# A selective scan with its carry moved out of the scan: one bundle of changes to a Mamba and FFN layer on one core

## The chip, the cores and the metric

The kernel runs on one NeuronCore of one Trainium2 chip. The engines are named PE (matrix products; PEld is its weight load), DVE (the vector engine), ACT (the scalar engine), POOL (GpSimd) and SP (which only issues DMAs here). SBUF is the on-chip memory, PSUM the smaller one that PE writes its sums to; a tile is 128 partitions by so many columns. The metric is the device time of one execution in microseconds (us). Before the change it is 2003.3 us, the median of three runs (2002.98, 2003.30 and 2004.07).

## What is computed

The input x is [2, 4096, 256]. One layer is a state-space block with a residual, then an FFN with a residual, in fp32 throughout. Cut to what matters here:

```python
x_path, z = split(layernorm(x) @ W_in.T)      # 512 channels each
x_path = silu(x_path)
B, C, dt_in, lam_in = split(x_path @ W_x.T)   # 16 states
B, C = rope(rmsnorm(B + B_bias)), rope(rmsnorm(C + C_bias))
dt = softplus(dt_in * W_dt + b_dt)            # 512 channels
dA = exp(A * dt)                              # 512 channels x 16 states
u = (1 - lam) * dt * dA * Bx_prev + lam * dt * Bx    # Bx = B * x_path
h[t] = dA[t] * h[t-1] + u[t]                  # the scan, along 4096 tokens
y[t] = sum over states (h[t] * C[t])
y = (y + x_path * D) * silu(z)
x = x + layernorm(y @ W_out.T)
o = ffn(layernorm(x))       # ternary weights, gelu, an inner layernorm
x = x + layernorm(o)
```

The scan is the part that can't be cut along time: 2 batches x 512 channels x 16 states, each 4096 steps long.

## The kernel before, in words

Time is cut into blocks of 512 tokens, 8 to a batch, 16 in all (`k`). The 512 channels x 16 states of a block are laid out as 4 channel groups `j` x 4 state rounds `q` x 4 quarters `c`: a tile of 128 partitions holds 32 channels of quarter `c` for 4 states, and its 512 columns are the tokens. So a block has 64 units, each with one scan, and a batch's later blocks start their scans from the last state of the block before. Blocks 0 and 8 start a batch and have no carry.

For each unit:

- `decay` (L1036): ACT writes exp(A dt) into a PSUM tile `da`; there are 4 such buffers (`DA_PSUM`). The call is the helper at L230.
- `inputs` (L1041, the product with B): POOL multiplies the broadcast row b with the channel tile `vr` into the SBUF tile `g`, two quarters at a time (L1046). There are 3 buffers of g, one per (j, q) (`GBUFS`).
- `unit_scan` (L1052): DVE scans. Its start value is 0 in the first block of a batch and a column of `ini` otherwise. The first `SPLIT[q]` quarters (2, 1, 2, 1) are scanned into `da` in PSUM (L1059), the others into g (L1062).
- The product with C: for quarters in PSUM DVE does it, `product_v` (L1074, with a copy of the last state into `hl` at L1077); for quarters in g POOL does it in place, `product_g` (L1068, L1072). In place, it overwrites the last state, so `last` (L1064) has ACT copy that to `hl` first.
- `sum_states` (L1084): PE adds the 16 states of a channel into PSUM (L1088), which frees g. `start_y` puts the skip term there first, `gate` (DVE, L1098) multiplies with silu(z).

The carry: `over`, `over_x`, `spread` and `carry` (L943 to L1027) bring what the last token of the block before adds to this block's first inputs into `ini`; `initial` (POOL, L1032) adds the last states `hl`. It is called from the main loop, once for j = 0 and once for the rest.

Around the scan of block k run, on the same engines, the preparation of block k+1 (`plan_ahead`: norm, projections, dt, angles of the rotation, rotation, loads) and the output projection and FFN of block k-1 (`plan_behind`). At its end `ffn_scale` (ACT, L1220) scales the FFN's output by its norm's factor and `finish` (POOL, L1224) adds it to x, which is then stored.

The order of the work is written out by hand. `tc.manual_schedule()` keeps the program's order on each engine; each engine takes its instructions in that order and waits with semaphores. The main loop goes through the units, and each unit has three places (3 x unit, + 1, + 2); the scan stands between the second and the third. `AT` gives for each piece of the two plans the place, counted from the start of the current block (192 places a block), behind which it is written down; `AT_FIRST` does so for the first block's preparation, `W_AT` for the ternary weights, and `LAG` for the pieces that follow a unit (products, sums, gates) counts from the unit's own place. Decays and inputs come by `ahead`: at the middle place of each unit, decays are issued up to 2 units ahead and inputs too (`AHEAD_DA`, `AHEAD_U`). Loads of dt and v for channel group j+1 are issued when group j starts, and x two blocks on at unit 60 (`X_AT`). SP issues all block loads and stores from one queue, in that order as well.

The tiles b and c are two columns longer than the data, which starts at column 2, so that POOL's two inputs start 8 bytes apart modulo 32 bytes; the rows of g, before the change, have 512 columns and are written and read at the same address.

Of the kernel before, what the change touches and what calls it, by code (L numbers as in the profile page):

```python
# [8 lines left out]
F32 = mybir.dt.float32  # L9
# [5 lines left out]
P = 128  # L15
# [30 lines left out]
AHEAD_DA, AHEAD_U = 2, 2  # L46
X_AT = 60
# [4 lines left out]
    "product_v": (4,),  # L52
    "last": (24, 15, 21, 18, 13, 13, 18, 14, 19, 21, 21, 14, 15, 13, 19, 11),
    "product_g": (28, 17, 30, 19, 22, 17, 20, 26, 24, 21, 25, 20, 24, 13, 24, 15),
    "gate": (35, 38, 31, 26),
    "start": (18, 26, 27, 26),
    "sum": (32, 30, 36, 25, 36, 35, 24, 30, 31, 29, 28, 23, 45, 31, 29, 22),
}

W_AT = (1, 46, 70, 73, 74, 78, 85, 92, 103, 103, 106, 114, 116, 124, 141, 144, 149, 149, 153, 160, 160, 163, 163, 170, 174, 176, 180, 187, 188)  # L60
LOAD_FIRST = 6
AT = {
    "a_stats": (5, 5),
    "a_power": (5,),
    "a_offset": (8,),
    "a_apply": (8, 8),
    "a_turn": (15, 15),
    "a_evict": (16, 17),
    "project": (17, 24, 31, 31, 62, 66, 66, 76),
    "keep": (21, 25, 31, 35, 68, 72, 74, 78),  # L70
    "silu_x": (36,),
    "bc_project": (55, 60),
    "bc_take": (73,),
    "dt_project": (82,),
    "bc_square": (88,),
    "bc_power": (95,),
    "dt_row": (84,),
    "dt_spread": (92,),
    "softplus": (92,),
    "bc_scale": (137,),  # L80
    "dt_turn": (109, 115, 117, 117),
    "dt_keep": (117, 118, 118, 120),
    "dt_sum": (121,),
    "angles": (129,),
    "diag_lam": (118,),
    "silu_z": (153,),
    "sines": (153,),
    "rotate_a": (154,),
    "rotate_b": (154,),
    "bc_turn": (158,),  # L90
    "bc_store": (164,),
    "dot_sum": (176,),
    "dot_shift": (194,),
    "dot_take": (194,),
    "weigh": (141, 159, 194, 196),
    "weigh_x": (150, 167, 197, 197),
    "over": (121,),
    "over_x": (132,),
    "spread": (179,),
    "carry": (185,),  # L100
    "diag_dot": (196,),
    "skip": (198, 199, 199, 200),
    "skip_x": (198, 199, 200, 200),
    "load_dt": (124,),
    "load_v": (150,),
    "load_b": (167, 172, 172, 174),
    "load_c": (172, 184, 186, 189),
    "x_load": (4,),
    "out_project": (41, 49),
    "out_square": (47, 49),  # L110
    "out_power": (49, 54),
    "residual": (53, 54),
    "h_stats": (58, 58),
    "h_power": (63,),
    "h_offset": (65,),
    "h_apply": (68, 69),
    "h_turn": (78, 82),
    "h_evict": (78, 82),
    "ffn_1": (85, 93, 97, 98, 103, 107, 117, 129),
    "ffn_keep": (88, 94, 97, 106, 114, 115, 121, 135),  # L120
    "gelu": (133, 135),
    "ffn_2": (137, 150, 162, 190),
    "ffn_sums": (145, 159, 173, 191),
    "ffn_out": (146, 159, 175, 195),
    "ffn_square": (177, 160, 195, 196),
    "ffn_power": (180, 196),
    "ffn_scale": (189, 196),
    "finish": (189, 196),
# [3 lines left out]
    "a_stats": (-90, -90),  # L132
    "a_power": (-90,),
    "a_offset": (-90,),
    "a_apply": (-90, -90),
    "a_turn": (-90, -90),
    "a_evict": (-90, -90),
    "project": (-78, -77, -75, -72, 0, 12, 0, 3),
    "keep": (-76, -74, -71, -69, 0, 16, 0, 9),
    "silu_x": (-58,),  # L140
    "bc_project": (-70, -70),
    "bc_take": (-67,),
    "dt_project": (-66,),
    "bc_square": (-61,),
    "bc_power": (-60,),
    "dt_row": (-65,),
    "dt_spread": (-64,),
    "softplus": (-63,),
    "bc_scale": (-59,),
    "dt_sum": (-53,),  # L150
    "dt_turn": (-55, -55, -55, -55),
    "dt_keep": (-55, -55, -55, -55),
    "angles": (-52,),
    "diag_lam": (-54,),
    "silu_z": (56,),
    "sines": (-50,),
    "rotate_a": (-47,),
    "rotate_b": (-46,),
    "bc_turn": (-45,),
    "bc_store": (-44,),  # L160
    "dot_sum": (-30,),
    "dot_shift": (0,),
    "dot_take": (0,),
    "weigh": (-51, 0, 0, 2),
    "weigh_x": (-49, 0, 4, 8),
    "diag_dot": (0,),
    "skip": (1, 9, 0, 0),
    "skip_x": (2, 12, 0, 0),
    "load_dt": (-62,),
    "load_v": (-42,),  # L170
    "load_b": (-43, -20, 0, 7),
    "load_c": (-41, -20, 5, 20),
    "bc_project_first": (-73, -70, -69, -68),
    "decay_rates": (-57,),
# [4 lines left out]
def mamba_ffn_kernel(  # L179
# [374 lines left out]
    class Norm:  # L554


        def __init__(self, src, scale, eps, name):
            self.src, self.scale, self.eps, self.name = src, scale, eps, name
            self.mv = small.tile([P, NC4, 2], F32, tag="mv", name=f"mv_{name}")
            self.st = small.tile([P, NC4, 6], F32, tag="st", name=f"st_{name}")  # L560

        def stats(self, cs):
            for c in cs:
                nc.vector.bn_stats(self.st[:, c, :], self.src[:, c, :])
                nc.vector.bn_aggr(self.mv[:, c, :], self.st[:, c, :])
# [21 lines left out]
        def turn(self, kk):  # L587
            if kk == 0:
                self.oT = p1.tile([P, 2, T], F32, tag="oT", name=f"oT_{self.name}")
                self.pt = {}  # L590
# [1018 lines left out]
```

## Time and profile before

| what | value |
|---|---|
| median of three runs | 2003.3 us |
| span of the profiled execution | 2000.2 us (its own time beside it isn't given; the runs' median stands 3.1 us above the span) |
| one steady block (64 scans) | 116.5 us |
| first scan of block 0 / of block 1 | 59.8 / 196.1 us after the start |
| granted PE clock, mean | 0.953 |
| DVE: all 1024 scans | 1270 us of 1766 us busy |
| POOL: `inputs` and `product_g` | 1016 and 628 us of 1750 us busy |
| ACT: decays | 680 us of 1625 us busy |

How to read it. A profile line of a group gives the line in the kernel, the engine, the operation, the tile written and the tiles read (`out<-in`, buffer numbers left out), the shapes, how often it ran, then the busy time in us, the mean of one in ns, and the idle time of the engine just before these instructions with what ended most of it. Busy time that overlaps is counted once per group; neighbouring DVE instructions overlap by some 0.07 us. A line of a wait names who waited for whom, the us in total, the times and the longest. A line of the timeline is the start in us, the length in us, and the instruction. In the table of windows each engine has its busy us and its instructions in brackets; behind them stand the granted clock, the DMA engines' busy share and GB/s.

### The profile page before, as it was taken

The page shows a single profiled execution, that of the slowest core. Times are in us where ns is not written, and L with a number is a line of the kernel's source. Part 1 is how long each engine was busy: PE and PEld are TensorE (multiplying, and loading weights), DVE is VectorE, ACT ScalarE, POOL GpSimd, SP SyncE. Part 2 cuts the span into 40 slices and gives each one's busy share as a digit, 9 for nine tenths or more (in the row PEclk, how much of TensorE's full clock was granted, in tenths as well). Part 3 has the DMA queues.
Part 4 walks back from the last instruction along what each step waited for, and adds up shares of the span by engine and source line. Part 5 has one row for each costly group of instructions (what it writes and reads, how often), then busy time and mean ns, then how long its engine had stood idle before and what let it go on. Part 6 is the DMA issues. An engine that isn't in the chain of part 4 may idle for free.

```text
span 2000.2 us, 28645 instructions
## 1 busy us (share of the span) xinstructions
PE 1779.9 (89%) x8910; PEld 1058.4 (53%) x8910; DVE 1765.9 (88%) x2714; ACT 1625.3 (81%) x3511; POOL 1750.2 (88%) x1063
## 2 busy tenths in 40 slices
PE   6866999999999999999999999999999999998788
PEld 3433555464645546464554646455464645545257
DVE  1778989999898999999899999989999998999961
ACT  4766897979789797978979797988979798896754
POOL 3689999999899999999999999999999999999970
PEclk7876999999999999999999999999999999999898
DMA  5733446365354636545463644546364454635400
GB/s 98 194 85 100 113 113 169 79 153 123 101 123 112 166 78 155 126 102 122 113 170 86 157 111 109 126 113 162 85 160 106 113 125 111 161 85 149 85 21 11
DMA packets 155721, 233.41 MB, mean 117 GB/s; under 512 B 30160, under 2 KB 55824, under 8 KB 155568
## 3 DMA queue, kind: packets, MB, share of 16 engines
q1 hardware_dynamic: 153440, 230.80, 47.8%
q0 software_dynamic: 544, 0.71, 0.3%
q8 instruction: 70, 1.15, 0.3%
q14 instruction: 83, 0.68, 0.1%
q10 hardware_dynamic: 1584, 0.07, 0.1%
HBM read 188.51 MB, written 42.99 MB: 116 GB/s over the span
## 4 chain that ended last, share of the span: by engine, by line
DVE 41%; ACT 27%; PE 12%; issue 12%; POOL 3%; DMA 3%; SPq 0%; DVEq 0%; ACTq 0%; POOLq 0%
DVE g L1062 16%; DVE da L1059 12%; ACT da L230 7%; ACT L228 5%; DVE g L1076 4%; PE pf L1162 3%; ACT L230 2%; PE pz L644 2%; ACT dt L230 2%; POOL g L1046 2%; ACT zs L230 2%; DVE dx L989 1%; PE pf L1171 1%; DVE zs L1098 1%; ACT h L230 1%
## 5 line engine op out<-in xcount | busy, mean ns | idle before, releaser
L1046 POOL TENSOR_TENSOR g<-b,vr 128x1024 f32<-128x1024 f32 x512 | 1016.2, 2000 | 44.9 <-PE y L1088 22.5
L230 ACT ACTIVATE da<-dtr,aneg 128x512 f32<-128x512 f32 x1024 | 680.2, 681 | 33.6 <-DVE hl L1077 18.2
L1062 DVE TENSOR_TENSOR_SCAN g<-da,ini,g 128x512 f32<-128x512 f32 x560 | 688.4, 1267 | 19.8 <-ACT da L230 19.1
L1072 POOL TENSOR_TENSOR g<-c,g 128x1024 f32<-128x1024 f32 (+1 forms) x256 | 626.5, 2452 | 88.6 <-ACT hl L1066 69.1
L1059 DVE TENSOR_TENSOR_SCAN da<-da,ini,g 128x512 f32<-128x512 f32 x336 | 429.3, 1278 | 39.6 <-ACT da L230 32.9
L1088 PE MATMUL y<-g,fold 128*32 128x512 f32 x2048 | 339.7, 630 | 39.8 <-POOL g L1072 28.0
L1162 PE MATMUL pf<-w2q,h 128*128 128x257 f32 x1024 | 313.1, 387 | 15.5 <-DVE o L1200 11.8
L1076 DVE TENSOR_TENSOR g<-da,c 128x512 f32<-128x512 f32 x384 | 264.1, 688 | 17.6 <-DVE da L1059 0.5
L644 PE MATMUL pz<-oT_a,wi 128*128 128x512 f32 x512 | 243.3, 617 | 33.0 <-ACT zs L662 28.6
L1139 PE MATMUL ph<-oT_h,w1q 128*128 128x512 f32 x480 | 250.7, 654 | 22.0 <-ACT h L1150 17.1
L1171 PEld LDWEIGHTS pf<-h 128*128 128x128 f32 x1024 | 194.8, 190 | 26.9
L1171 PE MATMUL pf<-h 128*128 128x128 f32 x1024 | 196.9, 274 | 0.0
L1162 PEld LDWEIGHTS pf<-w2q,h 128*128 128x128 f32 x1024 | 155.2, 192 | 59.0 <-DVE o L1200 43.1
L644 PEld LDWEIGHTS pz<-oT_a,wi 128*128 128x128 f32 x512 | 91.5, 193 | 173.8 <-issue 74.3
L1139 PEld LDWEIGHTS ph<-oT_h,w1q 128*128 128x128 f32 x480 | 88.6, 202 | 178.5 <-issue 79.3
L1088 PEld LDWEIGHTS y<-g,fold 128*32 128x32 f32 x2048 | 53.3, 110 | 176.7 <-POOL g L1072 82.9
L1066 ACT COPY hl<-g 128x2 f32<-128x2 f32 (+1 forms) x256 | 47.0, 184 | 104.4 <-DVE g L1062 100.1
L228 ACT ACT_TABLE_LOAD x98 | 125.7, 1283 | 1.7
L1108 PE MATMUL po<-wo,zs 128*128 128x256 f32 x480 | 112.8, 389 | 0.0
L1108 PEld LDWEIGHTS po<-wo,zs 128*128 128x128 f32 x480 | 89.7, 192 | 37.1 <-ACT xp L662 11.8
L928 PE MATMUL ps<-dt,ident 128*128 128x511 f32 x128 | 73.0, 654 | 28.8 <-DVE remdot L890 25.1
L1062 DVE TENSOR_TENSOR_SCAN g<-da,g 128x512 f32<-128x512 f32 x80 | 93.7, 1207 | 2.7 <-ACT da L230 2.6
(232 smaller groups left out, 2460.2 us busy)
## 6 DMA issues: line engine op xcount, KB each, us to landing
dtr<-dt_d SPq DMA_DIRECT2D x256, 256.0 KB, 4.8
vr<-v_d SPq DMA_DIRECT2D x256, 256.0 KB, 7.3
dt_d<-dt SPq DMA_DIRECT2D x64, 256.0 KB, 2.1
v_d<-v SPq DMA_DIRECT2D x64, 256.0 KB, 2.8
b<-bc_d SPq DMA_DIRECT2D x256, 64.0 KB, 2.1
c<-bc_d SPq DMA_DIRECT2D x256, 64.0 KB, 2.2
xpre<-in_L_attn_x_dram SPq DMA_DIRECT2D x16, 512.0 KB, 4.4
xpost<-in_L_attn_x_dram SPq DMA_DIRECT2D x15, 512.0 KB, 4.6
```

Source lines behind the costliest of these rows:

```text
L228: nc.scalar.preload_act_table_set(name)
L230: nc.scalar.activation(dst, src, f, **kw)
L644: nc.tensor.matmul(s.pz[e], lhsT=wi[:, kk, e * P : (e + 1) * P], rhs=s.na.oT[:, kk, :], start=(kk == 0), stop=(kk == 1),)
L1046: nc.gpsimd.tensor_mul(s.g[j, q][:, hs, :], s.bcq[0, q][:, None, :].to_broadcast([P, 2, T]), s.ch[j, "vr"][:, hs, :],)
L1059: nc.vector.tensor_tensor_scan(da, da, g, ini, ALU.mult, ALU.add)
L1062: nc.vector.tensor_tensor_scan(g, da, g, ini, ALU.mult, ALU.add)
L1072: nc.gpsimd.tensor_mul(g, s.bcq[1, q][:, None, :].to_broadcast([P, NG - n, T]), g)
L1076: nc.vector.tensor_mul(s.g[j, q][:, c, :], da, s.bcq[1, q])
L1088: nc.tensor.matmul(s.ys[j][c * G : (c + 1) * G, :], lhsT=fold, rhs=g[:, c, :], start=False, stop=(q == NQ - 1), skip_group_check=True,)
L1139: nc.tensor.matmul(s.ph[f], lhsT=w1q[:, kk, f * P : (f + 1) * P], rhs=s.nh.oT[:, kk, :], start=(kk == 0), stop=(kk == 1),)
L1162: nc.tensor.matmul(po[:, 0 : DM + 1], lhsT=gT, rhs=w2q[:, f, :], start=(f == 0), stop=(f == NH - 1), skip_group_check=True,)
L1171: nc.tensor.matmul(po[:, DM + 1 :], lhsT=gT, rhs=gT, start=False, stop=False, skip_group_check=True,)
```

## The change

Seven things change together.

1. `inputs` makes all four quarters of a round in one POOL instruction of 128x4x512 instead of two.
2. The rows of g get 514 columns. `inputs` writes columns 2 to 513, the scan works there, and both products with C write columns 0 to 511, two columns ahead of what they read. Column 513, the last state, stays as it was, so `product_g` need not follow `last`.
3. Every scan starts from 0. A new piece `enter` (DVE) adds the carry to the first column of the four quarters before the scan, 16 times a block. For this the carry is multiplied with the first decay: `over_x` also copies the first dt, `spread` spreads it, `carry` makes `da0` from it (one DVE multiplication, one exponential), and `initial` has a second POOL multiplication.
4. `ffn_scale` is gone. `finish` is a DVE instruction a quarter of the block, which scales and adds at once, in place of ACT's scaling and POOL's addition.
5. `angles` is cut into 7 pieces with places of their own, the statistics of the norms are issued two by two, the four dt tiles are one.
6. Decays, inputs, `enter`, `initial`, the loads of dt and v and the load of the next x get places in the tables; `AHEAD_DA`, `AHEAD_U`, `X_AT` and `LOAD_FIRST` are gone.
7. Nearly all places in `LAG`, `AT`, `AT_FIRST` and `W_AT` are new.

The core of the diff:

```diff
-    def inputs(s, j, q, h):
-
-        if h == 0:
-            s.g[j, q] = scan.tile([P, NG, T], F32, tag="g", name=f"g_{s.k}_{j}_{q}", bufs=GBUFS)
-        hs = slice(2 * h, 2 * h + 2)
+    def inputs(s, j, q):
+
+        s.g[j, q] = scan.tile([P, NG, T + 2], F32, tag="g", name=f"g_{s.k}_{j}_{q}", bufs=GBUFS)
         nc.gpsimd.tensor_mul(
-            s.g[j, q][:, hs, :],
-            s.bcq[0, q][:, None, :].to_broadcast([P, 2, T]),
-            s.ch[j, "vr"][:, hs, :],
+            s.g[j, q][:, :, 2:],
+            s.bcq[0, q][:, None, :].to_broadcast([P, NG, T]),
+            s.ch[j, "vr"],
         )
 
+    def enter(s, j, q):
+
+        g0 = s.g[j, q][:, :, 2]
+        nc.vector.tensor_add(g0, s.ini[:, j, q, :], g0)
+
     def unit_scan(s, j, q, c):
 
-        da, g = das[s.k, j, q, c], s.g[j, q][:, c, :]
-        ini = 0.0 if s.first else s.ini[:, j, q, c : c + 1]
+        da, g = das[s.k, j, q, c], s.g[j, q][:, c, 2:]
...
-            nc.vector.tensor_tensor_scan(da, da, g, ini, ALU.mult, ALU.add)
+            nc.vector.tensor_tensor_scan(da, da, g, 0.0, ALU.mult, ALU.add)
...
-        nc.scalar.copy(s.hl[:, j, q, n:], s.g[j, q][:, n:, T - 1])
+        nc.scalar.copy(s.hl[:, j, q, n:], s.g[j, q][:, n:, T + 1])
...
-        nc.gpsimd.tensor_mul(g, s.bcq[1, q][:, None, :].to_broadcast([P, NG - n, T]), g)
+        nc.gpsimd.tensor_mul(
+            g[:, :, 0:T], s.bcq[1, q][:, None, :].to_broadcast([P, NG - n, T]), g[:, :, 2:]
+        )
...
-        nc.vector.tensor_mul(s.g[j, q][:, c, :], da, s.bcq[1, q])
+        nc.vector.tensor_mul(s.g[j, q][:, c, 0:T], da, s.bcq[1, q])
...
+        s.da0 = scan.tile([P, NJ, NQ, NG], F32, tag="da0", name=f"da0_{s.k}")
+        nc.vector.tensor_mul(s.da0, dt0[:, :, None, :].to_broadcast([P, NJ, NQ, NG]), aneg)
+        special(s.da0, s.da0, AF.Exp)
...
         nc.gpsimd.tensor_add(s.ini[:, js], s.ini[:, js], prev.hl[:, js])
+        nc.gpsimd.tensor_mul(s.ini[:, js], s.ini[:, js], s.da0[:, js])
...
-    def ffn_scale(s, h):
-        for i in range(2):
-            o = s.o2[:, 2 * h + i, :]
-            nc.scalar.activation(o, o, AF.Copy, scale=s.ff["rg", h][:, i : i + 1])
-
     def finish(s, h):
         hs = slice(2 * h, 2 * h + 2)
-        nc.gpsimd.tensor_add(s.x[:, hs, :], s.o2[:, hs, :], s.x[:, hs, :])
+        for i in range(2):
+            c = 2 * h + i
+            xc = s.x[:, c, :]
+            nc.vector.scalar_tensor_tensor(
+                xc, s.o2[:, c, :], s.ff["rg", h][:, i : i + 1], xc, ALU.mult, ALU.add
+            )
         nc.sync.dma_start(tokens(out, s.k)[:, hs, :], s.x[:, hs, :])
```

And of the places (after the change, in order of j, q and, for decays, c):

```diff
-AHEAD_DA, AHEAD_U = 2, 2
-X_AT = 60
...
+    "decay": (-3, -4, 0, -3, -7, 1, 1, 0, -2, -1, 0, 0, -1, 1, -17, -3, ...
+    "inputs": (-9, -2, -7, -2, -7, -19, -11, 1, -11, -6, -11, -2, -9, -11, -2, -8,),
+    "enter": (-1, 1, -3, -1, 1, 0, 0, 1, -3, -1, -2, 1, -1, 0, 1, -1,),
...
-    "product_g": (28, 17, 30, 19, 22, 17, 20, 26, 24, 21, 25, 20, 24, 13, 24, 15),
+    "product_g": (18, 19, 13, 17, 12, 20, 14, 13, 16, 19, 18, 11, 27, 14, 24, 13,),
...
-    "x_load": (4,),
+    "x_load": (33,),
...
+    "initial": (181, 220,),
+    "x_next": (185,),
-    "load_dt": (124,),
-    "load_v": (150,),
+    "load_dt": (149, 200, 232, 264,),
+    "load_v": (173, 224, 234, 274,),
```

## The prediction

> **What bounds the kernel now.** I read the busy times first, then one steady block, then the groups of instructions with shapes kept apart, then the waits, then the timeline where DVE and POOL meet.
>
> The page's head:
>
> ```profile
> span 2000.2 us, 28645 instructions
> PE 1779.9 (89%) x8910; PEld 1058.4 (53%) x8910; DVE 1765.9 (88%) x2714; ACT 1625.3 (81%) x3511; POOL 1750.2 (88%) x1063
> ```
>
> No engine stands out, so the steady block decides. The timeline has the first scans of blocks 5, 6 and 7 at 663.1, 779.6 and 896.1 us: 116.5 us a block, and within 0.2 us of it for eleven of the fifteen intervals. The busy times of one such window (after the length: PE, PEld, DVE, ACT, POOL):
>
> ```profile
> 779.60:896.10 116.50, 108.11 (x554) 63.94 (x554) 109.66 (x169) 100.13 (x216) 107.94 (x65) 0.99 0.52 124
> ```
>
> DVE has 6.9 us a block unused, PE and POOL 8.5, ACT 16. DVE is nearest to its end, so what a block costs DVE is what the change is worth; POOL comes next. The groups (busy us, mean ns of one, idle before):
>
> ```profile
> L1046 POOL TENSOR_TENSOR g<-b,vr 128x1024 f32<-128x1024 f32 x512 | 1016.2, 2000 | 44.9 <-PE y L1088 22.5 <-DMA c<-bc_d 12.4 <-DVE hl L1077 8.7
> L1062 DVE TENSOR_TENSOR_SCAN g<-da,ini,g 128x512 f32<-128x512 f32 x560 | 688.4, 1267 | 19.8 <-ACT da L230 19.1 <-POOL g L1046 0.6
> L1059 DVE TENSOR_TENSOR_SCAN da<-da,ini,g 128x512 f32<-128x512 f32 x336 | 429.3, 1278 | 39.6 <-ACT da L230 32.9 <-POOL g L1046 6.7
> L1062 DVE TENSOR_TENSOR_SCAN g<-da,g 128x512 f32<-128x512 f32 x80 | 93.7, 1207 | 2.7 <-ACT da L230 2.6
> L1059 DVE TENSOR_TENSOR_SCAN da<-da,g 128x512 f32<-128x512 f32 x48 | 58.6, 1220 | 13.1 <-POOL g L1046 9.7 <-ACT da L230 3.2
> L1072 POOL TENSOR_TENSOR g<-c,g 128x1536 f32<-128x1536 f32 x128 | 371.9, 2905 | 65.8 <-ACT hl L1066 63.6 <-ACT dtc L721 1.9 <-DMA vr<-v_d 0.3
> L1072 POOL TENSOR_TENSOR g<-c,g 128x1024 f32<-128x1024 f32 x128 | 255.7, 1998 | 22.8 <-DMA vr<-v_d 10.2 <-issue 6.1 <-ACT hl L1066 5.5
> L1224 POOL TENSOR_TENSOR xpost<-o,xpost 128x512 f32<-128x512 f32 x30 | 32.7, 1088 | 7.4 <-ACT o L1220 6.3 <-DMA b<-bc_d 1.0
> L1220 ACT ACTIVATE o<-o,rsg 128x256 f32<-128x256 f32 x60 | 27.2, 501 | 0.5
> L1304 DVE SCALAR_TENSOR_TENSOR x_last<-o,rg,x_last 128x256 f32<-128x256 f32 x4 | 1.9, 484 | 4.6 <-ACT rg L230 4.6
> L425 POOL TENSOR_TENSOR wide<-wide 128x1024 f32<-128x1024 f32 x4 | 9.4, 2349 | 0.0
> ```
>
> To see: a scan that starts from a carry in SBUF costs 60 ns more than one from 0 (1267 to 1207, 1278 to 1220); POOL costs about 190 ns a call and 1.77 ns a column ((2905-1998)/512). Two waits the change aims at or lives with:
>
> ```profile
> POOL g L1072 <- ACT hl L1066: 69.1, 63, 2.1
> DVE da L1059 <- ACT da L230: 36.1, 30, 1.9
> ```
>
> And the place where DVE and POOL meet, two DVE instructions of one kind, with POOL's beside the second:
>
> ```profile
> 110.69 1.26 DVE L417 TENSOR_SCALAR wide<-wide,scale 128x2048 f32<-128x2048 f32 x1
> 161.02 3.69 DVE L417 TENSOR_SCALAR wide<-wide,scale 128x2048 f32<-128x2048 f32 x1
> 160.72 2.91 POOL L1072 TENSOR_TENSOR g<-c,g 128x1536 f32<-128x1536 f32 x1
> 163.59 2.98 POOL L1046 TENSOR_TENSOR g<-b,vr 128x1024 f32<-128x1024 f32 x1
> 1.62 0.32 DVE L263 TENSOR_TENSOR fold<-fold,ident 128x32 f32<-128x32 f32 x1
> ```
>
> Alone, L417 takes 1.26 us. At 161.02 POOL is inside a product that ends at 163.63; L417 ends 1.1 us after that, and POOL's next call needs 2.98 instead of 2.00. So DVE waited out the whole POOL call, then POOL waited for DVE. L417 and its sister L420 read and write SBUF only. All large DVE work in the steady blocks has one tensor in PSUM, and each scan form keeps within 20 ns of its mean beside a POOL that is always busy. DVE instructions with two tensors in SBUF occur before the change only in the set-up and the tail; of three equal adds in the set-up, the one that ran beside a POOL read took 0.32 us (L263), the others 0.19.
>
> **The change, part by part, for one block of 64 scans.**
>
> *Scans from 0.* 64 x 0.060 = -3.8 us of DVE, in the 14 blocks that carry a state.
>
> *The carry (`enter`).* 16 adds of 128x4, strided. L958 and L890 (128x4) take 135 and 153 ns: 16 x 0.15 = +2.4 us. One multiplication for `da0` (L1023's 0.2 us). Running beside nothing that is +2.6.
>
> *Other residual (`finish`).* POOL loses 2 x 1.09 = 2.2 us, ACT 4 x 0.50 = 2.0, DVE gains 4 x 0.484 = +1.9 (L1304). DVE's instructions alone: -3.8 + 2.6 + 1.9 = +0.7 us a block.
>
> *One product with B a group.* 16 calls of 2048 columns, 190 + 2048 x 1.77 = 3.81 us, for 32 of 2.00: -3.0 us of POOL. Two small multiplications in `initial` return 0.5. POOL: 107.9 - 3.0 - 2.2 + 0.5 = 103.2.
>
> *Products two columns ahead.* The last column of g survives, so POOL no longer waits for ACT's copy: 69.1 us of POOL idle may go, 4.6 a block. Late next is the sum on PE, which frees the g buffer (22.5 us before L1046). The new alignment of rows could cost: at worst every column at L425's rate, (2349-190)/1024 = 2.11 ns, 8 x 0.35 + 8 x 0.52 = +7 us of POOL; at best nothing. I take nothing, as 1.77 holds for both shapes of L1072, and in the sum POOL has room for either.
>
> *What the carry waits for.* `enter` and `finish` are the first steady DVE instructions with two tensors in SBUF: 16 + 4 a block. Their wait is not in the trace. One end is 0 (L1304 in the tail, 484 ns, POOL silent). The other is a whole POOL call: L417 lost 3.69 - 1.26 = 2.43 us, a longer call would take up to 3.81. L263 (+0.13 us) is nearest in kind, but its POOL call lasts 0.55 us; L417 is nearest in size of what it meets, so I take its rule, what is left of POOL's call. In the trace the mean rest of POOL's call when a group's first scan starts is 1.08 us (224 groups, 99% find POOL busy). Arrival at random gives the sum of squares over twice the sum: (32x2.00² + 8x2.91² + 8x2.00²)/(2x103.2) = 1.10, so random is right here. With the new lengths it is (16x3.81² + 8x2.91² + 8x2.00²)/(2x100.3) = 1.65. Times POOL's share of the longer block, 107/139 = 0.77 (103.2 and about 4 that DVE's turns hold it up): 1.27 us. 20 x 1.27 = +25.4 us a block on DVE, in front of every scan of the group, with ACT's PSUM buffers and PE's sums queued behind.
>
> The order on each engine speaks for a little less and for more. Carry (2,0) stands straight behind a scan on which POOL's product also waits: no wait. Carry (1,2) has 0.7 us of `product_v` between, and POOL starts the 2.9 us product of (1,1) first: 2.2 us. Carry (2,1) meets the 3.81 us call for (2,2) that began half a microsecond earlier: 3.3. Ten of the 16 stand straight behind a scan. Walking groups (1,1) to (3,3) so with row durations gives a mean of 1.35.
>
> *A rule on this.* The Trainium skill's page "SBUF — State Buffer", section "Who interferes with whom", says that a DVE instruction with two SBUF inputs contends with a GpSimd instruction that reads SBUF, and that the second to issue blocks until the first has ended. L417 shows the whole-call wait for another kind; that two inputs do it, only L263 hints. By the rule the sum is the one below; by L1304's row alone it would be some 1980.
>
> *Placement.* Decays go out up to 17 places (5.7 scans) early: ACT has 16 us a block free, and only four PSUM buffers, so cost nothing; if that cover goes, the copies and keeps behind a waiting decay on ACT are late and PE behind them. On SP, x for the next block now stands ahead of the loads of b for rounds 1 to 3 (before: ahead of c's), and waits for PE's last FFN product; b lands in 2.1 us and is needed about then. `load_v` 1 is issued 9 places (9 x 116.5/192 = 5.5 us) before its product, `load_v` 0 10 places, against 7.3 us to land: 0 to 3 us a block together. I take 0, since a slower block stretches the places. x_load goes from place 4 to 33, 14 places (8.5 us) before its use against 4.6 to land: hidden. The split of `angles` moves its eight instructions and adds none. The set-up is reordered: block 0 takes 136.3 us, 19.8 over a steady one, so 0 to -10; I take 0.
>
> **Sum.** +0.7 + 25.4, less about 4 of DVE's 6.9 us of gaps (mostly waits for ACT and POOL, which now come early) = +22.1 us; 14 blocks: +309. The block with no carry: 4 x 1.27 + 1.9 - 3 = +4 (its scans start from 0 already). 2000.2 + 313 = 2313 span; the median of the runs stands 3.1 us over the profiled span: about 2316.
>
> **Rivals.**
> 1. *The carries run beside POOL* (other side). Then DVE is +0.7 and POOL -4.7, with its waits for `hl` gone. If gaps fall from 6.9 to 3 us: 113.3 a block, 15 x -3.2 = -48, 1955; if they stay, +10, 2013. Middle 1980. It decides below a mean wait of (4 - 0.7)/20 = 0.17 us each. For it: L263 lost 0.13. Against: L417.
> 2. *DVE and POOL fall into step.* With DVE slow, POOL has often finished and waits for the same scan; the ten carries straight behind a scan go free, six pay 1 to 2 us, the finishes 1.27 each: 11 to 17, less 4, plus 0.7: +8 to +14 a block, 2115 to 2200. Speaks for it: the carry of (2,0); against: POOL's order often has two products with B ready to run.
> 3. *Rows align badly or loads come late*, with no blocking: +7 on POOL gives 110.2, still under DVE; 3 us of late v gives 15 x 2 = +30 at most: 2003 to 2035.
>
> **How the numbers follow.** Blocking with random arrival 0.57 (its own range 2200 to 2390), in step 0.17, free and faster 0.20, rival 3 0.06. Under 0.2% (4 us) a measurement of this kernel can't tell a change: half of rival 3. Slower: 0.57 + 0.17 + 0.03 = 0.77. The range from 1970 to 2385 leaves out the lower part of rival 1 and the tail above.
>
> **What would show it.** Right: the carry's add, 150 ns of work, lasting 1 to 1.5 us on average and up to 4 beside POOL, `finish` 1.5 instead of 0.48; scans at 1.21; POOL calls of 3.8 us; POOL's share falling to some 77%, blocks of about 139 us. Wrong: carries of 150 to 200 ns with POOL busy, or products with C well over 2.0 and 2.9 us. The blocking step is what makes the forecast: if it fails, rival 1 stands.

## The result, and the profile after

The changed kernel takes 2208.6 us (median of four runs, 2205.3 to 2211.8) against 2003.7 for the kernel before: a ratio of 1.102 [1.101, 1.104]. It is 205 us slower; 313 were forecast. The profiled execution spans 2205.2 us.

The head of the page of the changed kernel (busy us, share of the span, instructions), and the chain that ended last by engine:

```profile
span 2205.2 us, 28220 instructions
PE 1854.6 (84%) x8910; PEld 1120.6 (51%) x8910; DVE 2006.7 (91%) x3012; ACT 1612.7 (73%) x3480; POOL 1741.1 (79%) x805
DVE 54%; PE 16%; ACT 13%; POOL 8%; issue 4%; DMA 3%; SPq 2%; POOLq 0%; DVEq 0%; ACTq 0%
```

DVE is busy 241 us longer. PE is busy 75 us longer, at a granted clock of 0.912 in place of 0.953; ACT and POOL are busy 13 and 9 us less. The first scan starts at 56.5 us (before 59.8). The blocks with a carry last 129.0 to 132.9 us, 130.9 on average (before 116.5). Of the two without one, block 8 lasts 115.0 us (before 113.8) and block 0, in which the set-up still runs, 140.6 (before 136.3). So nearly all of the loss lies in the blocks with a carry, 14 x 14.4 = 202 us.

The groups of the changed kernel, shapes kept apart (busy us, mean ns of one, idle before and what ended it):

```profile
L1058 POOL TENSOR_TENSOR g<-b,vr 128x2048 f32<-128x2048 f32 x256 | 977.5, 3822 | 180.0 <-PE y L1106 69.2 <-issue 43.3 <-ACT hl L1082 27.9
L1078 DVE TENSOR_TENSOR_SCAN g<-da,g 128x512 f32<-128x512 f32 x640 | 763.1, 1207 | 24.6 <-ACT da L231 24.4
L1075 DVE TENSOR_TENSOR_SCAN da<-da,g 128x512 f32<-128x512 f32 x384 | 461.8, 1217 | 33.6 <-ACT da L231 20.4 <-POOL g L1058 9.1
L1088 POOL TENSOR_TENSOR g<-c,g 128x1536 f32<-128x1536 f32 x128 | 395.0, 3086 | 173.5 <-DVE g L1067 89.2 <-DVE g L1078 61.3 <-DMA vr<-v_d 17.7
L1088 POOL TENSOR_TENSOR g<-c,g 128x1024 f32<-128x1024 f32 x128 | 279.2, 2181 | 9.8 <-DVE g L1067 8.4 <-DVE g L1078 1.4
L1067 DVE TENSOR_TENSOR g<-ini,g 128x4 f32<-128x4 f32 x224 | 295.8, 1321 | 17.7 <-POOL g L1058 17.7
L1238 DVE SCALAR_TENSOR_TENSOR xpost<-o,rsg,xpost 128x256 f32<-128x256 f32 x60 | 36.1, 642 | 1.2 <-ACT rsg L231 1.2
```

To see: the scans are at 1.21 as forecast. The carry's add, four elements in each partition, takes 1.32 us on average and 296 us in all. POOL's calls with B last 3.82 us (forecast 3.81), its products with C 0.18 us more than before. POOL no longer waits for ACT's copy of the last column before it multiplies with C (69.1 us before). It waits for DVE instead, and the view puts 97.6 us of this down to the add:

```profile
POOL g L1088 <- DVE g L1067: 97.6, 42, 3.9
```

One of these 42 waits in the timeline, with POOL's idle time in brackets:

```profile
589.71 1.21 DVE L1078 TENSOR_TENSOR_SCAN g<-da,g 128x512 f32<-128x512 f32 x1
590.85 0.13 DVE L1067 TENSOR_TENSOR g<-ini,g 128x4 f32<-128x4 f32 x1
591.00 3.08 POOL L1088 TENSOR_TENSOR g<-c,g 128x1536 f32<-128x1536 f32 x1 [3.91 <-DVE g L1067]
```

In all 42 the add took 0.13 to 0.15 us and stood straight behind a scan, and the product started 0.08 us after that scan had ended (0.14 in two). The same product starts 0.08 to 0.15 us after its scan in no_carry_add, where there is no add at all. So what POOL waits for here is the scan, its input, and the add is only the last instruction that ended before it.

All instructions of the add (duration min/median/max in ns), and two of them in the timeline with what POOL did (start us, us, ..., xcount; POOL's rows join neighbouring calls):

```profile
L1067 DVE TENSOR_TENSOR g<-ini,g x224: 132/712/3764, 195.2 to 2135.0; 128x4 f32<-128x4 f32 x112
```

```profile
627.85 5.22 POOL L1088 TENSOR_TENSOR g<-c,g 128x1536 f32<-128x1536 f32 x2
630.25 0.71 DVE L1067 TENSOR_TENSOR g<-ini,g 128x4 f32<-128x4 f32 x1
671.50 7.59 POOL L1058 TENSOR_TENSOR g<-b,vr 128x2048 f32<-128x2048 f32 x2
675.42 3.69 DVE L1067 TENSOR_TENSOR g<-ini,g 128x4 f32<-128x4 f32 x1
```

The first add starts 0.69 us before POOL's first call of the two ends (627.85 + 3.09 = 630.94) and lasts 0.71. The second starts just after the second of two calls has begun; that one ends at 679.09, the add at 679.11. I matched all 224 adds with POOL's instructions in the trace: 85 found POOL idle and took 0.144 us; 139 found it in a call with 2.018 us left on average, and took 2.040. They end 0.02 us after the call.

### The profile page after: what moved, and what is told of

Read it like the earlier page. It is cut to its first block, busy times and chain, and to the rows that moved or that the text cites. A ratio compares the mean times of both kernels' runs of the same rounds, so it can differ in the third digit from the quotient of the medians.

```text
span 2205.2 us, 28220 instructions
## 1 busy us (share of the span) xinstructions
PE 1854.6 (84%) x8910; PEld 1120.6 (51%) x8910; DVE 2006.7 (91%) x3012; ACT 1612.7 (73%) x3480; POOL 1741.1 (79%) x805
## 4 chain that ended last, share of the span: by engine, by line
DVE 54%; PE 16%; ACT 13%; POOL 8%; issue 4%; DMA 3%; SPq 2%; POOLq 0%; DVEq 0%; ACTq 0%
DVE g L1078 18%; DVE g L1067 12%; DVE da L1075 10%; POOL g L1058 5%; DVE g L1094 5%; ACT da L231 4%; PE pz L649 3%; PE pf L1179 3%; ACT L229 2%; PE ph L1157 2%; POOL g L1088 2%; PE y L1106 2%; PE pf L1188 1%; SPq L1007 1%; ACT xp L231 1%
## 5 line engine op out<-in xcount | busy, mean ns | idle before, releaser
L1058 POOL TENSOR_TENSOR g<-b,vr 128x2048 f32<-128x2048 f32 x256 | 977.5, 3822 | 180.0 <-PE y L1106 69.2
L1088 POOL TENSOR_TENSOR g<-c,g 128x1024 f32<-128x1024 f32 (+1 forms) x256 | 672.7, 2634 | 183.3 <-DVE g L1067 97.6
L1078 DVE TENSOR_TENSOR_SCAN g<-da,g 128x512 f32<-128x512 f32 x640 | 763.1, 1207 | 24.6 <-ACT da L231 24.4
L1075 DVE TENSOR_TENSOR_SCAN da<-da,g 128x512 f32<-128x512 f32 x384 | 461.8, 1217 | 33.6 <-ACT da L231 20.4
L1106 PE MATMUL y<-g,fold 128*32 128x512 f32 x2048 | 350.5, 655 | 86.6 <-ACT y L1100 39.7
L1067 DVE TENSOR_TENSOR g<-ini,g 128x4 f32<-128x4 f32 x224 | 295.8, 1321 | 17.7 <-POOL g L1058 17.7
L649 PE MATMUL pz<-oT_a,wi 128*128 128x512 f32 x512 | 255.5, 639 | 9.0 <-DVE xpost L1150 7.5
L923 PE MATMUL pw<-ddot,dtT 128*128 128x128 f32 (+1 forms) x512 | 106.6, 372 | 70.0 <-ACT ddot L908 53.7
L923 PEld LDWEIGHTS pw<-ddot,dtT 128*128 128x128 f32 x512 | 91.8, 264 | 104.6 <-ACT ddot L908 68.1
L1209 ACT ACTIVATE mf<-pf 128x1 f32<-128x1 f32 x64 | 10.7, 167 | 149.1 <-DVE junk L1205 148.6
```

Source lines behind the costliest of these rows:

```text
L649: nc.tensor.matmul(s.pz[e], lhsT=wi[:, kk, e * P : (e + 1) * P], rhs=s.na.oT[:, kk, :], start=(kk == 0), stop=(kk == 1),)
L1058: nc.gpsimd.tensor_mul(s.g[j, q][:, :, 2:], s.bcq[0, q][:, None, :].to_broadcast([P, NG, T]), s.ch[j, "vr"],)
L1067: nc.vector.tensor_add(g0, s.ini[:, j, q, :], g0)
L1075: nc.vector.tensor_tensor_scan(da, da, g, 0.0, ALU.mult, ALU.add)
L1078: nc.vector.tensor_tensor_scan(g, da, g, 0.0, ALU.mult, ALU.add)
L1088: nc.gpsimd.tensor_mul(g[:, :, 0:T], s.bcq[1, q][:, None, :].to_broadcast([P, NG - n, T]), g[:, :, 2:])
```

## The experiments

Each run with what it left of a block: the mean length of blocks 2 to 14 (one of the 13 has no carry), and in it the time that DVE and POOL were busy, overlaps counted once. Times are medians; the kernel before, measured anew beside them, took 2001.6 to 2003.9 us, and the ratios go by that.

| run | time us | ratio to before | block us | DVE busy | POOL busy |
|---|---|---|---|---|---|
| kernel before | 2003.7 | | 116.4 | 109.3 | 107.8 |
| changed kernel | 2208.6 | 1.102 [1.101, 1.104] | 129.5 | 124.4 | 107.2 |
| no_carry_add | 1998.7 | 0.998 [0.997, 0.999] | 115.3 | 108.4 | 107.1 |
| psum_operand | 2007.2 | 1.003 [1.002, 1.004] | 116.6 | 109.5 | 107.1 |
| carry_on_pool | 2018.7 | 1.009 [1.008, 1.011] | 117.1 | 108.5 | 110.1 |
| carry_as_start | 2018.2 | 1.009 [1.007, 1.010] | 117.2 | 111.5 | 106.7 |
| half_calls | 2151.7 | 1.075 [1.073, 1.077] | 126.0 | 120.7 | 109.6 |
| rows_apart | 2171.8 | 1.084 [1.079, 1.088] | 126.8 | 122.9 | 104.5 |
| old_residual | 2153.2 | 1.074 [1.073, 1.076] | 125.4 | 119.5 | 109.0 |
| carry_on_pool_rows | 1995.3 | 0.997 [0.996, 0.998] | 115.7 | 108.1 | 107.2 |
| carry_on_pool_old_residual | 2002.2 | 0.999 [0.998, 1.000] | 116.1 | 104.6 | 108.9 |
| add_in_before | 2532.3 | 1.265 [1.263, 1.267] | 151.2 | 125.3 | 108.5 |
| psum_in_before | 2296.3 | 1.146 [1.144, 1.148] | 135.2 | 108.8 | 108.5 |
| columns_in_before | 2004.1 | 1.000 [0.999, 1.001] | 116.4 | 109.2 | 107.8 |

### The add left out

```diff
-        "enter": lambda s, j, q, c: None if s.first else enter(s, j, q),
+        "enter": lambda s, j, q, c: None,
```

> The changed kernel with the 224 carry additions (enter) left out, so that no block takes over the state of the one before; all other work and every place stay. Theory A (the additions wait out POOL's calls, 295.8 us of DVE in 224 additions, 21.1 us a block): the block falls from 130.9 us to 113 to 117, the time to 1960 to 2010 us. Theory B (the new places or the longer POOL calls make the block long, and the additions only show where DVE would have waited anyway): 2150 us or more, with the time reappearing as waits of scans for POOL or ACT. Theory C (the residual on DVE): 2150 or more as well, with finish at 0.64 us.

1998.7 us. Without the add no state passes from block to block. All 205 us hang on it, but without it the rest of the change gains only 0.2% (3 us). DVE's block is shorter by 0.9 us and its rest stays at 7.0 us: the gaps that the prediction thought would close do not close by themselves.

### One operand in PSUM

The first operand is four columns of a decay tile that lies in PSUM: the oldest one still in use, or, if there is none, the one made last (`made[-1]`). The kernel leaves out the carry; all else stays.

```diff
+        made[:] = [da]
...
-        nc.vector.tensor_add(g0, s.ini[:, j, q, :], g0)
+        da = next(iter(das.values()), made[-1])
+        nc.vector.tensor_add(g0, da[:, 0:NG], g0)
```

> The changed kernel with the carry addition kept on DVE, at its place, with the same shape and the same wait for POOL's product with B, but its first operand is four columns of a decay tile in PSUM in place of the carry in SBUF (so the state is not carried over). Theory A (only two tensors in SBUF make it wait): an addition takes 0.13 to 0.2 us whatever POOL does, the time falls to 1975 to 2020 us. Theory B (the strided addition is slow in itself, or it waits for the product with B): still about 1.3 us each, 2170 to 2220 us.

2007.2 us. The same add, as often, in the same place of the order, with the same destination in SBUF. All of its instructions in this kernel:

```profile
L1069 DVE TENSOR_TENSOR g<-da,g x224: 130/154/169, 195.6 to 1937.7; 128x4 f32<-128x4 f32 x112
```

and one beside POOL in the timeline of the same kernel:

```profile
616.23 5.22 POOL L1090 TENSOR_TENSOR g<-c,g 128x1024 f32<-128x1024 f32 x2
616.31 0.17 DVE L1069 TENSOR_TENSOR g<-da,g 128x4 f32<-128x4 f32 x1
```

The longest of 224 takes 0.17 us, and 175 of them started inside a POOL call that had 2.11 us left on average. Against the changed kernel 201 us are gone. So it is the second operand in SBUF that makes DVE wait for POOL's call, not the add, its place, its strides or its destination. The adds themselves fell by 262 us (295.8 - 34.0), DVE's busy time by 236 (2006.7 to 1770.8) and the kernel by 201. Most of the first difference is that the residuals now meet POOL's calls more fully (60 x 0.40 us, 0.64 to 1.04); the second is DVE's gaps, 5.1 us a block in the changed kernel and 7.2 here.

### The add on POOL

```diff
         nc.gpsimd.tensor_mul(
             s.g[j, q][:, :, 2:],
...
         )
+        if not s.first:
+            g0 = s.g[j, q][:, :, 2]
+            nc.gpsimd.tensor_add(g0, s.ini[:, j, q, :], g0)
...
-        "enter": lambda s, j, q, c: None if s.first else enter(s, j, q),
+        "enter": lambda s, j, q, c: None,
```

> The changed kernel with the carry addition on POOL, directly behind the product with B of its group, instead of DVE. POOL gets 16 calls of some 0.21 us more a block (0.20 us for 128x4), +3.4 us. Theory A: DVE's 21 us a block go, the block falls to 113 to 117 us, 1955 to 2010 us. Theory B (places, longer POOL calls): 2170 us or more, as POOL has more to do and nothing else changes.

2018.7 us, over the range. The adds of this kernel and the two shapes of the product with C:

```profile
L1065 POOL TENSOR_TENSOR g<-ini,g 128x4 f32<-128x4 f32 x224 | 47.1, 210 | 17.6
L1091 POOL TENSOR_TENSOR g<-c,g 128x1536 f32<-128x1536 f32 x128 | 395.4, 3089 | 25.2 <-DVE g L1081 19.6 <-DMA vr<-v_d 5.2 <-issue 0.3
L1091 POOL TENSOR_TENSOR g<-c,g 128x1024 f32<-128x1024 f32 x128 | 279.4, 2183 | 1.4 <-DVE g L1081 1.4
```

Two things on POOL cost it: 16 x 0.21 = 3.4 us of adds a block, and 16 x 0.18 = 2.9 us of slower products. POOL is now nearest to its end, 110.1 of 117.1.

### The carry as the start of the scan again

```diff
-        s.da0 = scan.tile([P, NJ, NQ, NG], F32, tag="da0", name=f"da0_{s.k}")
...
-        nc.gpsimd.tensor_mul(s.ini[:, js], s.ini[:, js], s.da0[:, js])
...
+        ini = 0.0 if s.first else s.ini[:, j, q, c : c + 1]
...
-            nc.vector.tensor_tensor_scan(da, da, g, 0.0, ALU.mult, ALU.add)
+            nc.vector.tensor_tensor_scan(da, da, g, ini, ALU.mult, ALU.add)
```

(both scans, and no `enter`.)

> The changed kernel with the carry given to the scans as their start value, as before the change: no carry addition, no multiplication with the first decay; all else and every place stay. Theory A: scans back at 1267 and 1278 ns (+3.8 us a block), the additions' 21 us gone: 115 to 119 us a block, 1985 to 2030 us, that is about the time before the change. Theory B: 2150 us or more.

2018.2 us. The scans are back at their old durations, 1268 and 1278 ns, and DVE at 111.5 us a block: the 60 ns come with a start value in SBUF, and this kernel is 2018.2 - 2007.2 = 11 us slower than the one whose adds are free of POOL. Part (3) of the change was sound in its aim; the way in which the carry enters undid it.

### Rows of 516 columns

The rows of g get 516 columns with the state in columns 2 to 513, and the tile of C starts at column 0 instead of 2.

```diff
-            t = scan.tile([P, T + 2], F32, tag="bc"[m], name=f"{'bc'[m]}_{s.k}_{q}", bufs=4)
+            o = 2 - 2 * m
+            t = scan.tile([P, T + o], F32, tag="bc"[m], name=f"{'bc'[m]}_{s.k}_{q}", bufs=4)
...
-        s.g[j, q] = scan.tile([P, NG, T + 2], F32, tag="g", name=f"g_{s.k}_{j}_{q}", bufs=GBUFS)
+        s.g[j, q] = scan.tile([P, NG, T + 4], F32, tag="g", name=f"g_{s.k}_{j}_{q}", bufs=GBUFS)
```

> The changed kernel with rows of g of 516 columns in place of 514 and the tile of c without its two leading columns, so that the two inputs of POOL's product with C lie 8 bytes apart modulo 16 in every row; with 514 columns every second row has them alike. If that is why these calls went from 1998 and 2905 ns to 2181 and 3086, they are back at 2.00 and 2.91 us, POOL has 2.9 us a block less to do; the time falls by 0 to 15 us, since DVE is the bound. If writing two columns ahead is slow in itself, 2.18 and 3.09 stay.

2171.8 us, 37 lower where at most 15 were expected. The products with C of this kernel, and its adds:

```profile
L1089 POOL TENSOR_TENSOR g<-c,g 128x1536 f32<-128x1536 f32 x128 | 372.0, 2906 | 174.0 <-DVE g L1068 94.1 <-DVE g L1079 51.8 <-ACT da L231 11.7
L1089 POOL TENSOR_TENSOR g<-c,g 128x1024 f32<-128x1024 f32 x128 | 256.2, 2002 | 13.1 <-DVE g L1068 11.5 <-DVE g L1079 1.6
L1068 DVE TENSOR_TENSOR g<-ini,g 128x4 f32<-128x4 f32 x224 | 270.5, 1208 | 6.1 <-POOL g L1059 5.2
```

The durations of before are back, so the place of g's rows against C's was the cause of the 0.18 us. My expectation counted POOL's 2.9 us a block as covered; but the adds end with POOL's calls, and with the shorter calls the adds became shorter as well, 1.32 to 1.21 us (16 x 0.11 = 1.8 of the block's 2.7 us). When DVE waits for POOL's calls, POOL's time is DVE's.

The same rows with the add on POOL (both diffs together):

> The carry addition on POOL and rows of g that lie 8 bytes apart from c. With the addition on POOL alone POOL was busy 110.3 us of a block of 117 and the time was 2018.7 us. If POOL's products set that block, 2.9 us a block come back: 1975 to 2000 us, below the kernel before. If DVE or ACT set it, 2010 to 2020.

1995.3 us, inside the range and 0.3% under the kernel before. It is the lowest median found, but its ratio (0.996 to 0.998) overlaps that of the run without any add (0.997 to 0.999), which has the rows of 514. POOL is at 107.2 us a block.

### POOL's calls cut in two

```diff
-        nc.gpsimd.tensor_mul(
-            s.g[j, q][:, :, 2:],
-            s.bcq[0, q][:, None, :].to_broadcast([P, NG, T]),
-            s.ch[j, "vr"],
-        )
+        for h in range(2):
+            hs = slice(2 * h, 2 * h + 2)
+            nc.gpsimd.tensor_mul(
+                s.g[j, q][:, hs, 2:],
+                s.bcq[0, q][:, None, :].to_broadcast([P, 2, T]),
+                s.ch[j, "vr"][:, hs, :],
+            )
```

> The changed kernel with each group's product with B again as two POOL calls of half the columns, both at the group's place. If an addition waits out the call that POOL has in hand, its mean falls from 1.32 us to 0.8 to 1.1 (sum of squares over twice the sum: 1.14 us for calls of 2.0, 2.2 and 3.1 us, times a busy share near 0.87), the block by 4 to 8 us, the time to 2100 to 2165 us, although POOL has 3 us a block more to do. If it waits for POOL's work as a whole, or for the product with B, it gets no shorter: 2205 us or more.

2151.7 us. The add in this kernel:

```profile
L1069 DVE TENSOR_TENSOR g<-ini,g 128x4 f32<-128x4 f32 x224 | 232.7, 1039 | 17.9 <-POOL g L1060 16.8
```

The adds take 1.04 us on average; the rest of POOL's call that an add meets falls from 2.02 to 1.46 us, and adds end 0.02 us after it, as before. POOL is busy 2.4 us a block longer, and the kernel is still 57 us faster: the wait goes by the length of the call, which part (1) of the change had doubled.

### The residual of before

```diff
-        for i in range(2):
-            c = 2 * h + i
-            xc = s.x[:, c, :]
-            nc.vector.scalar_tensor_tensor(
-                xc, s.o2[:, c, :], s.ff["rg", h][:, i : i + 1], xc, ALU.mult, ALU.add
-            )
+        for i in range(2):
+            o = s.o2[:, 2 * h + i, :]
+            nc.scalar.activation(o, o, AF.Copy, scale=s.ff["rg", h][:, i : i + 1])
+        nc.gpsimd.tensor_add(s.x[:, hs, :], s.o2[:, hs, :], s.x[:, hs, :])
```

> The changed kernel with the residual of the kernel before (ScalarE scales, one GpSimd add of 128x512 per two tiles, VectorE does nothing). The changed kernel's trace has 60 residual instructions of 0.64 us on VectorE, 2.4 us per block. By the prediction's own step for it (1.5 us each, 5 to 6 us per block with the waits) it would fall by 70 to 90 us to 2120 to 2140. By the durations found it falls by at most 15 x 2.4 = 36 us, and GpSimd's 2.2 us per block for the two adds give some back: 2175 to 2210. VectorE has little rest in that kernel, so I take 2185.

2153.2 us, 55 lower: between my two cases. The 60 instructions themselves were 36 us of DVE, and the adds, which now meet POOL at other moments, take 1.14 us instead of 1.32 (41 us over all). Of these 77 us the kernel gained 55. What one instruction costs and what it does to the phase of the two engines can't be told apart by its own row.

The version of carry_on_pool_rows with this residual:

> The version of the run carry_on_pool_rows (1995 us) with the residual of the kernel before. There the 60 residual instructions took 1.05 us each on VectorE (4 us per block, since they met GpSimd's calls), while GpSimd is busy 107 us of 115 and ScalarE about 99. If VectorE is what sets that version's block, up to 2 us per block go: 1965 to 1990. If GpSimd sets it, its 2.2 us per block for the two adds come on top: 2005 to 2030. If no one engine does, 1990 to 2005; that is the likeliest to me, since the run without carries left VectorE 7 us of rest per block too.

2002.2 us. DVE's busy time falls by 3.5 us a block to 104.6, and the time does not fall: with the add off DVE, DVE's busy time does not set the block. POOL, 1.7 us a block busier than without this residual, is now the busiest engine, 108.9 of 116.1. Which chain of waits sets the block is left open here.

### The add in the order of before

The kernel before with the scans from 0 and the add of 128x4 ahead of a group's first scan (the carry multiplied with the first decay as in the changed kernel, its inputs in two POOL calls as they were, issued up to three units ahead instead of two).

```diff
+        if c == 0 and not s.first:
+            g0 = s.g[j, q][:, :, 0]
+            nc.vector.tensor_add(g0, s.ini[:, j, q, :], g0)
...
-            nc.vector.tensor_tensor_scan(da, da, g, ini, ALU.mult, ALU.add)
+            nc.vector.tensor_tensor_scan(da, da, g, 0.0, ALU.mult, ALU.add)
...
-AHEAD_DA, AHEAD_U = 2, 2
+AHEAD_DA, AHEAD_U = 2, 3
```

> The kernel before, with its own places, its residual and its products, changed in one point: scans from 0 and the carry added on DVE before the first scan of each group, 16 additions a block with both tensors in SBUF (the products with B go out one unit earlier, so that all four quarters are there; the first decay is multiplied in as in the change). Theory A: each addition lasts what is left of POOL's call; where a group's first scan starts that was 1.08 us in the trace before, so 1.0 to 1.2 us each, +10 to +13 us a block with the scans' -3.8, 2140 to 2190 us. Theory B (it needs the new places, or POOL's longer calls): 1970 to 2015 us, the additions at 0.15 us.

2532.3 us, some 340 over the range. The add in this kernel:

```profile
L1065 DVE TENSOR_TENSOR g<-ini,g 128x4 f32<-128x4 f32 x224 | 286.1, 1277 | 239.2 <-POOL g L1054 239.2
```

The lock is there as in the changed kernel (1.28 us an add, and again adds end 0.02 us after POOL's call). But there are 239 us more in front of it: the add needs all four quarters, and the order of before issues the second half of the inputs one unit ahead of the third scan; here it goes out one unit earlier, just ahead of the first scan, and the add waits for it. To tell the two apart I took the lock alone away:

```diff
-            nc.vector.tensor_add(g0, s.ini[:, j, q, :], g0)
+            nc.vector.tensor_add(g0, da[:, 0:NG], g0)
```

> The kernel of the run add_in_before, its adds in the same places and with the same waits, but the add's first operand is four columns of the decay tile in PSUM that is about to be scanned (so the carries are not passed on: that part of the computation is left out). Two causes for that run's 2532 us are told apart. Its trace has 224 adds of 1.28 us (286 us together) and, ahead of 101 of them, 239 us in which VectorE sat idle until GpSimd's second half of the inputs was there. If both are real, the lock goes and the order's wait stays: 2532 less 224 x (1.28 - 0.15) = 2279, and since a freed VectorE meets a GpSimd that is no faster, up to half of that wait could move, so 2180 to 2300. Had the lock made the wait as well (GpSimd late because VectorE was late), the time falls to the neighbourhood of the kernel before, 1990 to 2060. If two operands in SBUF do not matter here, it stays at 2500 or above.

2296.3 us. The add now:

```profile
L1065 DVE TENSOR_TENSOR g<-da,g 128x4 f32<-128x4 f32 x224 | 35.3, 158 | 309.7 <-POOL g L1054 309.7
```

Taking the lock away gained 236 us of the 529 (the adds' busy time fell by 251 us, while the wait ahead of them grew by 71). The 292 that stay go with the order: DVE sat idle 310 us for the second half. The lock without this wait was not run in the kernel before. The changed kernel has only 17.7 us of idle time ahead of its adds. Its one call a group is not what it takes: half_calls has two, both at the group's place, and 17.9 us. What is left to explain it is the new places, parts (6) and (7); they were not tried in the kernel before by themselves.

### The products two columns ahead alone

The kernel before with rows of 516 columns, C's tile from column 0 and both products written two columns ahead.

```diff
-            s.g[j, q] = scan.tile([P, NG, T], F32, tag="g", name=f"g_{s.k}_{j}_{q}", bufs=GBUFS)
+            s.g[j, q] = scan.tile([P, NG, T + 4], F32, tag="g", name=f"g_{s.k}_{j}_{q}", bufs=GBUFS)
...
-        nc.gpsimd.tensor_mul(g, s.bcq[1, q][:, None, :].to_broadcast([P, NG - n, T]), g)
+        nc.gpsimd.tensor_mul(
+            g[:, :, 0:T], s.bcq[1, q][:, None, :].to_broadcast([P, NG - n, T]), g[:, :, 2 : T + 2]
+        )
```

> The kernel before with only one part of the change: the products with C written two columns ahead of what they read, in rows of 516 columns (the placing and the carries stay as before). The prediction gave this part about 1 us per block of VectorE (688 to 672 ns for each of 24 products) and nothing on GpSimd: 1985 to 2003. If the part gives nothing because the block's length is set by the interplay of all four engines, as the run without carries said of the rest of the bundle, 1998 to 2006.

2004.1 us: no change. (The 672 ns in the expectation come from the changed kernel's trace; the prediction on record puts nothing of VectorE to this part.) The long product with C in this kernel:

```profile
L1073 POOL TENSOR_TENSOR g<-c,g 128x1536 f32<-128x1536 f32 x128 | 371.9, 2905 | 41.8 <-DVE g L1063 28.9 <-DMA vr<-v_d 7.1 <-POOL g L1073 3.9
```

The wait for ACT's copy is gone from this row (63.6 us before), and nothing comes of it: the product now waits for the scan on DVE itself, and POOL has 8.6 us of rest a block as before.

## Why the prediction was right, and where its sizes were not

The direction, the mechanism and the place held: `enter` waits out POOL's call, only in blocks with a carry, and it is the second tensor in SBUF that does it. Ahead of the result this was argued from L417, which reads one tensor from SBUF, and from L263, which is no clean case. POOL's call beside L263 was this one:

```profile
1.62 0.55 POOL L276 TENSOR_SCALAR deps<-ident 128x128 f32<-128x128 f32 x1
```

It ran to 2.17 us, and L263 had ended at 1.95, so L263 did not wait the call out. It is psum_operand that shows what the second tensor does.

The rule of the Trainium skill's page "SBUF — State Buffer", section "Who interferes with whom" (a DVE instruction with two inputs in SBUF and a GpSimd instruction that reads SBUF exclude each other, and the second to issue waits for the first), agrees with these runs: 2.04 us with both inputs in SBUF against 0.15 with one, both beside POOL.

The time, 2208.6, lies in the range and at the lower edge of the likeliest case's own (2200 to 2390). The range, 1970 to 2385, was wide, and the second rival ended at 2200, so the time alone would not tell these two apart; both have the wait in them, and the sum overstated the loss by half. Step by step, in us a block, where a block with a carry grew by 14.4 instead of 22.1:

| step | forecast | found |
|---|---|---|
| scans from 0 | -3.8 | -3.9 |
| the adds, own work and waits | 2.4 + 20.3 = 22.7 | 16 x 1.321 = 21.1 |
| `da0` | +0.2 | +0.2 |
| residual on DVE, own work and waits | 1.9 + 5.1 = 7.0 | 4 x 0.642 = 2.6 |
| product with C on DVE | 0 | 24 x -0.016 = -0.4 |
| records of neighbours that overlap | 0 | -2.5 |
| DVE's gaps | -4 | -2 (7.1 to 5.1) |
| sum | +22.1 | +15.1, against 14.4 measured |

- The step that failed most is "Times POOL's share of the longer block ... 1.27 us. 20 x 1.27", as far as it covers the four residuals. In this order 32 of the 60 find POOL idle and take 0.47 us, the others find on average 0.54 us left of a POOL call. The price of one that waits was nearer (0.48 + 1.65 = 2.13): in the run without the add, 30 of the 60 meet a call, with 1.44 us left, and take 1.74 us. Even there the mean of all 60 is 1.16 us, under the 1.75 of the sum (0.48 + 1.27).
- The mean for the add was right by two errors against each other. The rest of a call that an add meets is 2.02 us, not 1.65, and 62% of them meet one, not 77%. POOL is idle more often than its share says, because its product waits for the very scan on which DVE is: the 97.6 us above, and the 61.3 and 1.4 put down to the scan. That is what the second rival described, though at a smaller rate: at 7 of the 16 places the add takes under 0.5 us on average, at 9 between 0.7 and 3.7. Where the order was walked by hand, (1,2) came out near what was told (2.81 us; 2.2 of wait forecast), (2,0) and (2,1) did not (1.65 and 0.42; none and 3.3).
- An add that waits ends with the call, so its 0.15 us of work are inside the wait; the sum counted them on top. A residual that waits ends 0.28 us after the call, of the 0.47 us that it takes alone.
- "I take nothing" for the new rows was wrong by 2.9 us of POOL a block, of the 7 kept as the other end. It was held to be covered by POOL's rest; the run with 516 columns shows that it was not, since it also lengthens what DVE waits for.
- "Late next is the sum on PE": the wait for ACT's copy went, but late next was DVE's scan, ahead of the product with C. POOL's inputs still meet that copy, as the last reader of a g buffer (27.9 us in L1058's row).
- The first rival's 1955 (carries beside POOL, gaps closing to 3 us) is answered by psum_operand, 2007: with adds that do not wait, the kernel stands near that rival's upper end (2013), since the gaps stay at 7 us.
- The loads and decays in their new places, taken at 0, show no loss on balance: no_carry_add, with all of them, is 3 us under the kernel before.

## What to carry to other kernels

Before a small DVE instruction is put in front of a hot loop, count its tensors in SBUF: with two, its price here was what was left of GpSimd's current call (up to 3.74 us for four columns), and longer GpSimd calls raised that price. With one operand in PSUM, or on GpSimd itself, the same add cost 0.15 to 0.21 us here. And a part that must have all of a group's data at once needs an order that brings it: check both costs apart, since either was enough here to sink the change (205 us with the lock in the new order, 292 with the wait for data in the old one).

## What the runs showed of the hardware

- An add of 128x4 with both inputs in SBUF ends 0.02 us after the GpSimd call that it met, in five kernels (mean rests of 2.02, 1.67, 1.46, 1.85 and 1.48 us; 5% to 95% of the differences within 0.01 to 0.05). A residual of 128x256, also with both in SBUF, ends 0.28 us after it (0.28 to 0.32, all 28 that met a call in the changed kernel and all 30 in no_carry_add).
- GpSimd's product of two tensors in SBUF has two rates. With g in rows of 512 or 516 columns and C two columns off, both shapes go at 1.77 ns a column; with rows of 514 columns, each call takes 0.18 us more, which is one row of 512 columns at 2.11 ns ((2349-190)/1024, the rate of L425 before). Of two or three rows, one starts at the same remainder of 16 bytes as C. That this remainder is the cause is my reading of three widths of row; no run varied it further.
- The product with C on DVE takes 672 to 674 ns in the kernels with the new places and 688 in those with the old; writing two columns ahead does not bring it (688 in columns_in_before). In part it goes with what DVE did just ahead: behind a scan into g the product takes 664 ns (147 of 384 in the changed kernel, none before), behind a scan into PSUM before 692 (243 of 384). No run tested this.
- TensorE's granted clock was 0.953 before, 0.912 after, 0.925 in old_residual and 0.856 in add_in_before. The slower kernels have the lower clock, but pace is not all: no_carry_add, no slower than the kernel before, has 0.936. Its cause was not looked for.
